# Product 7 on the second Strassen level in two layers, and the first layer's value bias joined at its products

## The chip, the cores and the metric

The kernel runs on one core of one Trainium2 chip. Its engines work side by side, each through its own queue in order: TensorE (PE) multiplies matrices, VectorE (DVE), ScalarE (ACT) and GpSimd (POOL) work elementwise, and SyncE (SP) issues most DMA transfers. POOL issues the DMAs that add to what lies in DRAM. Matmul results land in PSUM, eight banks of 128 partitions by 512 float32 each; DVE and ACT read them out, POOL works in SBUF only.

The metric is the device time of the whole program in microseconds (us).

## The reference

Four layers work on x of shape (128, 64, 512): 128 graphs of 64 nodes with 512 features, all in float32. Each layer adds an attention over the graph's adjacency to x:

```python
h = maximum(layernorm(x), 0); x = x + L0(h, adj, Wq, bq, Wk, bk, Wv, bv)          # 8 heads of 64, softmax
h = maximum(layernorm(x), 0); x = x + L1(h, adj, Wq, bq, Wk, bk, Wv, bv, Wo, bo)  # the same, with an output product
h = maximum(layernorm(x), 0); x = x + L2(h, adj, Wq, Wk, Wv)                       # no softmax: scores masked, rows normed
h = maximum(layernorm(x), 0); x = x + L3(h, w_qkv, w_proj, b_proj, gamma, beta, adj)  # softmax, output product o, then o + layernorm(o)

# inside L0
q, k, v = x @ Wq + bq, x @ Wk + bk, x @ Wv + bv        # (n, 512) by (512, 512)
weights = softmax(q k^T / 8 + mask)                     # each row sums to one
out     = weights @ v
```

In layer 2 the products by Wq and Wk are folded into one 512 x 512 matrix a2 = Wq^T Wk ahead of time.

## The kernel before

**Tiles.** The 8192 rows are cut into NB = 16 blocks of T = 512 rows. The loop `for n in range(N)` near the end runs over N = 64 block-layers: n // 16 is the layer l, n % 16 the block k. A block is normed (`layer_norm`), turned so that features lie on partitions (`turn`: an ACT copy into a z tile that splits 32-bit words into halves, a DMA transpose on SP, an ACT copy back), and multiplied by the layer's weights (`projection`). Attention (`scores`, `attend`, `values`) or, in layer 2, `relate` follows, and x is stored.

**Products.** Each 512 x 512 x 512 product is done by Strassen's method in Winograd's form: the operands are cut into 2 x 2 quarters, eight additions make sums of quarters, and seven products replace eight. The weights' sums are made once a layer (`sums_w`), the block's sums once a block (`sums_x`, four POOL additions 512 wide into a tile S; SO for the output products). A first-level product, of 256 x 256 x 256, is four matmuls of 128 x 128 weights by 256 columns (`prod_T`, `prod_N`).

Some of the seven products are cut once more (`prod_2`): seven matmuls of 128 by 128 in place of four of 256. Which ones is the string that `finer` returns. Before, `LEVEL2` says "423" (products 4, 2 and 3) in layers 0, 1 and 3 from block 2 on, and "43" for the two products of layer 2, a2 and v2, which become "423" (`DEEP`) from block 2 of that layer. Each such product needs four more POOL additions 128 wide for the block (`sums_q`, whose results go to the list `room`) and four for the weight (`sums_q_w`; `deepen` calls it after block 1 of layer 2).

**How a projection runs.** `ORDERS` lists the steps. A number is a first-level product, a number in quotes the part of a deeper one that gathers in its own quarter, and "a", "b", "c" are the second-level terms that several quarters share. "423" runs as

```python
"423": (1, 5, 6, "a", 7, "b", "2", "c", "4", "3"),
"4237": (1, 5, 6, "7", "t", "a", "A", "2", "b", "B", "4", "c", "C", "3"),
```

The second line is already in the program, with the steps that it calls: "7" is three matmuls, "t" one whose result ACT copies to a tile p5 and POOL adds to a 256-wide pair, "A", "B" and "C" one each, which DVE adds 256, 256 and 512 wide. The results gather in PSUM banks named S, 5, T and 2; "A", "B" and "C" use a further one, D. DVE and ACT bring them to the result tile (qT, kT, v, xo), and POOL adds the p5 tiles. A bias is joined there: "col" by ACT's activation, "row" by a DVE add in place of the ACT copy for three quarters and a POOL add (`gps.tensor_tensor(Y[4], Y[4], wide(0), ALU.add)`) for the fourth. Layer 3's output product uses "row".

**Biases outside the products.** In layer 0 the value bias isn't added to v: since attention weights sum to one it is added to the residual, by four POOL additions 512 wide a block in `load_xo`. Layer 1's bo and layer 3's beta are held as a row on all partitions in SBUF and added to DRAM by POOL's accumulating DMAs, 1 MB a block (`adds`, `add_out`). These are the groups x<-row and out_dram<-row of the profile.

**Order.** Nothing is issued as it is written. Every call goes to a `Plan`, which records reads, writes and an estimated duration (`duration`) and then lists the steps by a simulation of the five queues and the eight banks (`order`): of the ready steps the one that could start first, ties by a rank from due times, moved by `PREFER`, a table of offsets in ns by kind of step. `HASTE` moves forward every step that reads a PSUM bank. `issue` emits the list, and so all instructions carry line 316 in the profile. The tables do not change what is computed.

**Buffers.** `Ring` hands out tiles in turn: z has 5, row 3, mx and sr 4, the p1 pool one tile a tag, S and hT two. A step that writes a tile waits for the last reader of what was in it.

Of the kernel before, what the change touches and what calls it, by code (L numbers as in the profile page):

```python
# [19 lines left out]
P = 128  # L20
G = 64
D = 512
# [319 lines left out]
class Pool:  # L342
# [34 lines left out]
ROOM = 5  # L377
DEEP = "423"
# [3 lines left out]
HASTE = 24970.0  # L382
# [5 lines left out]
    "gps dma_start out_0_dram<-row 2048": -808,  # L388
    "gps dma_start out_0_dram<-xo 2048": 3553,
    "gps dma_start x1<-kT 2": -2080,  # L390
    "gps dma_start x1<-row": 2529,
    "gps dma_start x1<-row 2": -1234,
    "gps dma_start x1<-xo": -129329,
    "gps dma_start x1<-xo 2": -25864,
    "gps memset mhalf<- 8": -5457,
    "gps tensor_scalar nb<-mv 4": 11572,
    "gps tensor_scalar nb<-mv 4 2": 33294,
    "gps tensor_scalar ve<-mv 1": -1763,
    "gps tensor_scalar ve<-mv 4": 11580,
    "gps tensor_scalar ve<-mv 4 2": -7060,  # L400
    "gps tensor_tensor S2<-S 128 2": 22107,
    "gps tensor_tensor S2<-S2 128": -559,
    "gps tensor_tensor S2<-S2 128 2": -54598,
    "gps tensor_tensor S2<-hT 128": 2551,
    "gps tensor_tensor S<-S 128": 1168,
    "gps tensor_tensor S<-S 128 2": 2476,
    "gps tensor_tensor S<-S 512": -597,
    "gps tensor_tensor S<-S 512 2": -7501,
    "gps tensor_tensor S<-hT 512": -24545,
    "gps tensor_tensor S<-hT 512 2": -3927,  # L410
    "gps tensor_tensor SO2<-SO 128": 4667,
    "gps tensor_tensor SO2<-SO 128 2": 15658,
    "gps tensor_tensor SO2<-SO2 128": 1209,
    "gps tensor_tensor SO2<-SO2 128 2": -10461,
    "gps tensor_tensor SO<-SO 128": -707,
    "gps tensor_tensor SO<-SO 128 2": -1689,
    "gps tensor_tensor SO<-SO 512": 11408,
    "gps tensor_tensor SO<-SO 512 2": 15673,
    "gps tensor_tensor SO<-oT 512": 1784,
    "gps tensor_tensor SO<-oT 512 2": 15975,  # L420
    "gps tensor_tensor hT<-hT 128": -1135,
    "gps tensor_tensor hT<-hT 128 2": 6337,
    "gps tensor_tensor kT<-kT 128": -30776,
    "gps tensor_tensor kT<-kT 128 2": -14217,
    "gps tensor_tensor kT<-kT 256": -12126,
    "gps tensor_tensor kT<-kT 256 2": -509,
    "gps tensor_tensor kT<-kT 512": 4991,
    "gps tensor_tensor nb<-nb 4": 378,
    "gps tensor_tensor nb<-nb 4 2": -22779,
    "gps tensor_tensor oT<-S 128 2": -2719,  # L430
    "gps tensor_tensor oT<-oT 128": -16598,
    "gps tensor_tensor oT<-oT 128 2": -20,
    "gps tensor_tensor qT<-qT 128": -1109,
    "gps tensor_tensor qT<-qT 128 2": -14844,
    "gps tensor_tensor qT<-qT 256": 8338,
    "gps tensor_tensor qT<-qT 256 2": 167,
    "gps tensor_tensor rn<-ss 8 2": 1409,
    "gps tensor_tensor row<-hT 128": -710,
    "gps tensor_tensor row<-row 128": 14918,
    "gps tensor_tensor rs<-ve 1": 27672,  # L440
    "gps tensor_tensor rs<-ve 4": 5403,
    "gps tensor_tensor rs<-ve 4 2": 2490,
    "gps tensor_tensor s<-hT 128 2": -24185,
    "gps tensor_tensor s<-s 1024": -91676,
    "gps tensor_tensor s<-s 128 2": -19641,
    "gps tensor_tensor v<-v 128": -3704,
    "gps tensor_tensor v<-v 128 2": -9488,
    "gps tensor_tensor v<-v 256": 1526,
    "gps tensor_tensor v<-v 256 2": 1506,
    "gps tensor_tensor w<-w 128": 28546,  # L450
    "gps tensor_tensor w<-w 128 2": 70002,
    "gps tensor_tensor w<-w 256": 2007,
    "gps tensor_tensor w<-w 512": 32937,
    "gps tensor_tensor w<-w 512 2": -1787,
    "gps tensor_tensor xo<-xo 128": 11193,
    "gps tensor_tensor xo<-xo 512": -37778,
    "sca activation kT<-mm 128": -29215,
    "sca activation kT<-mm 256": -3927,
    "sca activation qT<-mm 128": -74377,
    "sca activation qT<-mm 256": -3915,  # L460
    "sca activation s<-s 1024": 194087,
    "sca activation s<-s 256 2": -2224,
    "sca activation xin<-xin 512": 64227,
    "sca activation xin<-xin 512 2": -27076,
    "sca copy hT<-hp 1024": -91399,
    "sca copy hT<-hp 1024 2": 12660,
    "sca copy hT<-mm 512": 2537,
    "sca copy kT<-mm 128": -1201,
    "sca copy kT<-mm 128 2": 12050,
    "sca copy kT<-mm 256": 22596,  # L470
    "sca copy kT<-mm 512": 1630,
    "sca copy oT<-mm 512": 2583,
    "sca copy p5<-mm 128": -33327,
    "sca copy p5<-mm 128 2": -16443,
    "sca copy qT<-mm 128": 636,
    "sca copy qT<-mm 128 2": -1473,
    "sca copy qT<-mm 256": 1288,
    "sca copy qT<-mm 256 2": 7745,
    "sca copy qT<-mm 512 2": 1688,
    "sca copy s<-hp 1024": 10152,  # L480
    "sca copy s<-mm 512": 13393,
    "sca copy v<-mm 128": 2212,
    "sca copy v<-mm 128 2": -451,
    "sca copy v<-mm 256": -5758,
    "sca copy v<-mm 256 2": 10701,
    "sca copy v<-mm 512": 101913,
    "sca copy w<-mm 128": -125,
    "sca copy w<-mm 256": 8826,
    "sca copy xo<-mm 128": 19831,
    "sca copy xo<-mm 256": 6884,  # L490
    "sca copy xo<-mm 512": -3273,
    "sca copy z<-hp 1024": 9089,
    "sca copy z<-mm 512": 225,
    "sca copy z<-oT 1024": -34277,
    "sca copy z<-s 1024": 915,
    "sca copy z<-xin 1024": 71282,
    "sca copy z<-xin 1024 2": -375,
    "syn dma_start a2d<-z": 5859,
    "syn dma_start adj2<-in_adj_dram": -1388,
    "syn dma_start bk0<-in_L0_gnn_bk_dram": -130,  # L500
    "syn dma_start bk1<-in_L1_gnn_bk_dram": 5273,
    "syn dma_start bq0<-in_L0_gnn_bq_dram": 15019,
    "syn dma_start bq1<-in_L1_gnn_bq_dram": -1693,
    "syn dma_start bv1<-in_L1_gnn_bv_dram": -4763,
    "syn dma_start hp<-z": 10021,
    "syn dma_start hp<-z 2": -14842,
    "syn dma_start oT<-in_L2_gnn_Wq_dram": 7116,
    "syn dma_start oT<-in_L2_gnn_Wv_dram": 12239,
    "syn dma_start out_0_dram<-qT": -11288,
    "syn dma_start out_0_dram<-xo 2": 3308,  # L510
    "syn dma_start qT<-out_0_dram": -19349,
    "syn dma_start row<-in_L0_gnn_bv_dram": -4082,
    "syn dma_start row<-in_L1_gnn_bo_dram": 830,
    "syn dma_start row<-in_L3_gnn_b_proj_dram 2": 19121,
    "syn dma_start row<-in_L3_gnn_ln_gamma_dram 2": 15560,
    "syn dma_start w<-a2d": -573,
    "syn dma_start w<-in_L0_gnn_Wk_dram": 825,
    "syn dma_start w<-in_L0_gnn_Wq_dram": 17643,
    "syn dma_start w<-in_L0_gnn_Wv_dram": -7702,
    "syn dma_start w<-in_L1_gnn_Wo_dram": 2537,  # L520
    "syn dma_start w<-in_L1_gnn_Wq_dram": 10058,
    "syn dma_start w<-in_L1_gnn_Wv_dram": 14266,
    "syn dma_start w<-in_L3_gnn_w_proj_dram": 5411,
    "syn dma_start w<-in_L3_gnn_w_qkv_dram 2": 21150,
    "syn dma_start x1<-xo": -11230,
    "syn dma_start xin<-out_0_dram": -1632,
    "syn dma_start xin<-out_0_dram 2": -15870,
    "syn dma_start xin<-x1": -4553,
    "syn dma_start xo<-in_x_dram": 2298,
    "syn dma_start xo<-x1 2": 13243,  # L530
    "ten matmul mm<-S 128": 12919,
    "ten matmul mm<-S 128 2": 8018,
    "ten matmul mm<-S 256": 6187,
    "ten matmul mm<-S 256 2": -3891,
    "ten matmul mm<-SO 128": 3732,
    "ten matmul mm<-SO 128 2": 2595,
    "ten matmul mm<-SO 256": 281,
    "ten matmul mm<-SO 256 2": 3959,
    "ten matmul mm<-hT 128": 7158,
    "ten matmul mm<-hT 128 2": -5677,  # L540
    "ten matmul mm<-hT 256": 3637,
    "ten matmul mm<-hT 256 2": -7222,
    "ten matmul mm<-hT 64 2": 14063,
    "ten matmul mm<-oT 128": -2756,
    "ten matmul mm<-oT 256": -147,
    "ten matmul mm<-oT 256 2": -4195,
    "ten matmul mm<-oT 512": -5757,
    "ten matmul mm<-qT 64": 14482,
    "ten matmul mm<-row 128 2": -6474,
    "ten matmul mm<-s 128 2": 5537,  # L550
    "ten matmul mm<-s 256": 11122,
    "ten matmul mm<-s 256 2": 9177,
    "ten matmul mm<-s 64": 5357,
    "ten matmul mm<-v 64": -17945,
    "ten matmul mm<-v 64 2": -283,
    "ten matmul mm<-w 128": -1300,
    "ten matmul mm<-w 256": -118,
    "ten matmul mm<-w 256 2": 57,
    "ten transpose mm<- 128": 1068,
# [1172 lines left out]
```

## Time and profile before

| | before |
|---|---|
| median of 3 runs | 2752.95 us (2752.92 to 2753.37) |
| the profiled execution, its own time | 2752.1 us |
| its span | 2750.3 us |
| granted clock of TensorE | 0.999 |
| POOL, 16 DMAs x<-row (bo) of 1 MB, issue to landing | 13.9 us |
| POOL, 15 DMAs x<-xo of 1 MB, issue to landing | 9.2 us |
| SP, 444 transposes hp<-z, issue to landing | 3.3 us |
| ACT copies p<-mm 128 wide, 398 | 275 ns each |
| ACT copies v<-mm 512 wide, 194 | 596 ns each |
| DVE adds v<-mm,v 256 wide, 122 | 412 ns each |
| DVE adds v<-mm,v 512 wide, 314 | 687 ns each |

The span runs from the first instruction to the last one's end in the trace; what lies around it (1.8 us) belongs to the program's own time. PEld is TensorE's weight load, which overlaps its matmuls. POOL's records overlap each other by some 0.1 to 0.2 us, so what one of its instructions costs is read from start to start: four in a row, 128 wide, start at 1102.65, 1103.07, 1103.48 and 1103.90 us, 0.41 us apart, and two 256 wide take 1.40 us. A layer fills some 690 us of the span: the third starts at about 1461 us.

### The profile page before, as it was taken

The page shows a single profiled execution, that of the slowest core. Times are in us where ns is not written, and L with a number is a line of the kernel's source. Part 1 is how long each engine was busy: PE and PEld are TensorE (multiplying, and loading weights), DVE is VectorE, ACT ScalarE, POOL GpSimd, SP SyncE. Part 2 cuts the span into 40 slices and gives each one's busy share as a digit, 9 for nine tenths or more (in the row PEclk, how much of TensorE's full clock was granted, in tenths as well). Part 3 has the DMA queues.
Part 4 walks back from the last instruction along what each step waited for, and adds up shares of the span by engine and source line. Part 5 has one row for each costly group of instructions (what it writes and reads, how often), then busy time and mean ns, then how long its engine had stood idle before and what let it go on. Part 6 is the DMA issues. An engine that isn't in the chain of part 4 may idle for free.

```text
span 2750.3 us, 72249 instructions
## 1 busy us (share of the span) xinstructions
PE 2734.5 (99%) x29427; PEld 2506.0 (91%) x29427; DVE 1735.3 (63%) x3298; ACT 1897.0 (69%) x3169; POOL 2102.2 (76%) x2915
## 2 busy tenths in 40 slices
PE   9999999999999999999999999999999999999998
PEld 8999899999999999999999898989999999999997
DVE  6666566665656556556555555555577677677777
ACT  6788688888776766766766666665766666666662
POOL 5667778779978778778689866656887887887885
PEclk9999999999999999999999999999999999999999
DMA  5666576666465556465575856567544664754644
GB/s 143 157 149 133 148 151 146 154 143 164 80 124 110 93 115 110 94 115 107 97 150 123 179 146 169 151 154 181 113 90 81 119 114 78 127 105 84 130 88 97
DMA packets 635021, 344.50 MB, mean 125 GB/s; under 512 B 484288, under 2 KB 565952, under 8 KB 634688
## 3 DMA queue, kind: packets, MB, share of 16 engines
q1 hardware_dynamic: 601424, 273.83, 43.9%
q0 software_dynamic: 33264, 66.06, 14.7%
q8 instruction: 230, 3.77, 0.6%
q14 instruction: 103, 0.84, 0.1%
HBM read 120.63 MB, written 102.76 MB: 81 GB/s over the span
## 4 chain that ended last, share of the span: by engine, by line
PE 89%; POOL 6%; ACT 2%; DVE 1%; DMA 1%; issue 1%; SPq 0%; POOLq 0%; ACTq 0%; DVEq 0%
PE mm L316 89%; POOL w L316 2%; POOL s L316 1%; POOL S L316 1%; DMA hp<-z 1%; POOL SO L316 0%; ACT z L316 0%; ACT s L316 0%; DMA x<-xo 0%; ACT xin L316 0%; POOL xo L316 0%; ACT kT L316 0%; DVE st L316 0%; DVE sr L316 0%; POOL v L316 0%
## 5 line engine op out<-in xcount | busy, mean ns | idle before, releaser
L316 PE MATMUL mm<-S,w 128*128 128x256 f32 (+1 forms) x4516 | 900.1, 338 | 1.6 <-issue 1.0
L316 PEld LDWEIGHTS mm<-S,w 128*128 128x128 f32 x4516 | 734.5, 191 | 62.5 <-POOL S L316 1.0
L316 PE MATMUL mm<-hT,w 128*128 128x128 f32 (+1 forms) x3364 | 593.3, 307 | 0.8 <-ACT p L316 0.7
L316 PEld LDWEIGHTS mm<-hT,w 128*128 128x128 f32 x3364 | 509.8, 191 | 39.9 <-ACT p L316 1.4
L316 PE MATMUL mm<-w,S 128*128 128x256 f32 (+1 forms) x2520 | 514.9, 340 | 0.0
L316 DVE TENSOR_TENSOR kT<-mm,kT 128x256 f32<-128x256 f32 (+1 forms) x433 | 258.9, 612 | 317.1 <-PE mm L316 190.6
L316 PEld LDWEIGHTS mm<-w,S 128*128 128x128 f32 x2520 | 418.8, 191 | 42.0 <-ACT s L316 3.1
L316 DVE TENSOR_TENSOR v<-mm,v 128x512 f32<-128x512 f32 (+2 forms) x440 | 264.3, 607 | 232.1 <-PE mm L316 132.5
L316 DVE TENSOR_TENSOR qT<-mm,qT 128x512 f32<-128x512 f32 (+2 forms) x440 | 264.6, 609 | 196.7 <-PE mm L316 149.3
L316 ACT COPY hT<-hp 128x1024 uint16<-128x1024 uint16 x252 | 337.5, 1362 | 14.7 <-DMA hp<-z 14.3
L316 ACT COPY v<-mm 128x128 f32<-128x128 f32 (+1 forms) x380 | 172.2, 455 | 234.8 <-PE mm L316 205.4
L316 PE MATMUL mm<-w,hT 128*128 128x128 f32 (+1 forms) x1844 | 326.7, 307 | 1.1 <-DVE p L316 0.7
L316 PEld LDWEIGHTS mm<-w,hT 128*128 128x128 f32 x1844 | 277.8, 191 | 19.4 <-ACT s L316 0.9
L316 POOL TENSOR_TENSOR S<-hT 128x512 f32<-128x512 f32 (+1 forms) x172 | 196.3, 1219 | 104.8 <-ACT hT L316 104.8
L316 ACT COPY z<-xin 128x1024 uint16<-128x1024 uint16 x252 | 260.4, 1080 | 0.0
L316 POOL TENSOR_TENSOR qT<-qT,p 128x256 f32<-128x256 f32 (+1 forms) x184 | 118.0, 651 | 185.4 <-DVE qT L316 105.4
L316 PE MATMUL mm<-w,SO 128*128 128x256 f32 (+1 forms) x1302 | 259.1, 335 | 0.0
L316 ACT COPY s<-hp 128x1024 uint16<-128x1024 uint16 x188 | 253.0, 1373 | 1.6 <-DMA hp<-z 1.5
L316 POOL TENSOR_TENSOR s<-s,mx 128x1024 f32<-128x1024 f32 x96 | 208.5, 2221 | 40.9 <-DVE mx L316 40.7
L316 PEld LDWEIGHTS mm<-w,SO 128*128 128x128 f32 x1302 | 210.0, 191 | 16.8
L316 PE MATMUL mm<-w,oT 128*128 128x128 f32 (+1 forms) x1252 | 222.3, 303 | 0.2 <-ACT oT L316 0.2
L316 ACT COPY z<-s 128x1024 uint16<-128x1024 uint16 x188 | 193.7, 1053 | 39.5 <-POOL s L316 39.5
(125 smaller groups left out, 4811.5 us busy)
## 6 DMA issues: line engine op xcount, KB each, us to landing
xin<-x SPq DMA_DIRECT2D x128, 256.0 KB, 3.8
xin<-in_x_dram SPq DMA_DIRECT2D x64, 256.0 KB, 4.0
x<-row POOLq DMA_DIRECT2D x16, 1024.0 KB, 13.9
xin<-out_dram SPq DMA_DIRECT2D x64, 256.0 KB, 3.5
out_dram<-row POOLq DMA_DIRECT2D x16, 1024.0 KB, 13.9
x<-xo POOLq DMA_DIRECT2D x15, 1024.0 KB, 9.2
out_dram<-xo POOLq DMA_DIRECT2D x15, 1024.0 KB, 9.9
xo<-in_x_dram SPq DMA_DIRECT2D x32, 256.0 KB, 4.2
```

Of the source, the lines that this page charges most:

```text
L316: getattr(getattr(self.nc, eng), op)(*a, **k)
```

## The change

- **Product 7 deeper.** `DEEP` becomes "4237" and `finer` returns it for q1, k1, v1, a2 and v2 from block 2 of their layer on. Layers 0 and 3 and the output products keep "423".
- **Room for its sums.** `sums_x` hands out a second tile of eight 128-wide slots beside S (five before). `deepen` takes a tile for the weight's three sums, from a new ring w7 of two, or from the row ring for v1, and is now called in layer 1 too, after block 1. It makes the sums of product 7 (in layer 2 of products 2 and 7).
- **p5.** The tile of product 7 shares its buffer with that of product 2.
- **Layer 0's value bias** is passed to the projection as "row"; the four additions in `load_xo` are gone.
- **bo and beta** are no longer held in SBUF: the accumulating DMAs read them from DRAM, repeated over partitions.
- **Rings.** z goes from 5 tiles to 4, row from 3 to 2, mx and sr from 4 to 2; `fold`, which makes a2, uses the tiles of SO in place of z.
- **Order.** `PREFER` is replaced, with separate offsets for the four layers (before: layer 2 apart from the rest), and `HASTE` goes from 24970 to 60319. The other constants of the plan stay.

```diff
-ROOM = 5
-DEEP = "423"
+ROOM = {"S": 8, "SO": 5}
+DEEP = "4237"
+DEEPER = ("q1", "k1", "v1", "a2", "v2")
+LENT = ("v0", "v1")
...
-HASTE = 24970.0
+HASTE = 60319.0
...
-    zs, hps = pool("zs", 5), pool("hps", 4)
-    rows = pool("rows", 3)
-    sm = pool("sm", 4)
+    zs, hps = pool("zs", 4), pool("hps", 4)
+    rows, w7 = pool("rows", 2), pool("w7", 2)
+    sm, sm2 = pool("sm", 4), pool("sm2", 2)
...
     def finer(name, n):
-        if name[1] == "2" and n >= 2 * NB + 2:
+        if name in DEEPER and n % NB >= 2:
             return DEEP
...
-    def deepen(name, at):
-
-        if "rooms" not in W2:
-            W2["rooms"] = p1.tile([P, KC * KC, P], F32, tag="SO", name="rooms")
-        for i, q in enumerate("75"):
-            W2[name][q] = W2["rooms"][:, at + 3 * i : at + 3 * i + 3]
+    def deepen(name):
+
+        if name in LENT:
+            W2[name]["7"] = rows.tile([P, KC, P], F32, tag="row", name=f"w7_{name}")
+        else:
+            W2[name]["7"] = w7.tile([P, 3, P], F32, tag="w7", name=f"w7_{name}")
         for q in DEEP:
             if q not in LEVEL2[name]:
                 sums_q_w(name, q, gps.tensor_tensor)
...
-            f = zs.tile([P, D], F32, tag="z", name=f"fa_{dc}")
+            f = p1.tile([P, ROOM["SO"], P], F32, tag="SO2", name=f"fa_{dc}")[:, :KC].rearrange("p c f -> p (c f)")
...
-        if 3 * len(parts) > len(room):
-            more = (p2 if tag == "S" else p1).tile([P, ROOM, P], F32, tag=f"{tag}2", name=f"{nm}2")
-            room = room + [more[:, i] for i in range(ROOM)]
+        if 3 * len(parts) >= len(room):
+            more = (p2 if tag == "S" else p1).tile([P, ROOM[tag], P], F32, tag=f"{tag}2", name=f"{nm}2")
+            room = room + [more[:, i] for i in range(ROOM[tag])]
...
-            p5[q] = p1.tile([P, P], F32, tag=f"p5_{q}", name=f"p5_{q}_{nm}")
+            p5[q] = p1.tile([P, P], F32, tag=f"p5_{2 if q == '7' else q}", name=f"p5_{q}_{nm}")
...
-            mx = sm.tile([P, NS], F32, tag="mx", name=f"mx_{n}")
+            mx = sm2.tile([P, NS], F32, tag="mx", name=f"mx_{n}")
...
-        if l in xo_row:
-            row = R[xo_row[l]]
-            for t in range(NT):
-                gps.tensor_tensor(xos[n][:, t, :], xos[n][:, t, :], row, ALU.add)
-                if t < NT - 1:
-                    yield 1
         ready.add(("xo", n))
...
-            R["b1"] = row_bc("b1", bo1)
+            R["b1"] = bo1.partition_broadcast(P)
...
-            R["bp"], R["gam"], R["bet"] = row_bc("bp", bp3), row_bc("gam", gam3), row_bc("bet", bet3)
+            R["bp"], R["gam"], R["bet"] = row_bc("bp", bp3), row_bc("gam", gam3), bet3.partition_broadcast(P)
...
+            if k == 1 and f"q{l}" in DEEPER:
+                deepen(f"q{l}")
...
-            run(projection(prod_N, f"v{l}", xop, f"v_{n}", v))
+            run(projection(prod_N, f"v{l}", xop, f"v_{n}", v, (R["b0"][:, :H2], R["b0"][:, H2:]) if l == 0 else None))
+            if k == 1 and f"v{l}" in DEEPER:
+                deepen(f"v{l}")
```

## The prediction

> **What bounds the kernel now.** I read the busy times first, then the slices, the chain that ended last and TensorE's own waits. From the page:
>
> ```profile
> PE 2734.5 (99%) x29427; PEld 2506.0 (91%) x29427; DVE 1735.3 (63%) x3298; ACT 1897.0 (69%) x3169; POOL 2102.2 (76%) x2915
> PE   9999999999999999999999999999999999999998
> PEclk9999999999999999999999999999999999999999
> PE 89%; POOL 6%; ACT 2%; DVE 1%; DMA 1%; issue 1%; SPq 0%; POOLq 0%; ACTq 0%; DVEq 0%
> ```
>
> TensorE (PE) is busy in every slice at the full clock, and the chain is 89% matmul. Span less busy time is 2750.3 - 2734.5 = 15.8 us. The windows put 2.1 us of that into the first 43 us and 10.9 us into the last 86 us; only 2.8 us lies in between. Busy matmuls are modelled, so I ask next who ever kept PE waiting (engine <- what it waited for: us in total, times, longest):
>
> ```profile
> PE mm L316 <- issue: 1.5, 2, 1.0
> ...
> PE mm L316 <- DVE v L316: 1.0, 2, 0.7
> PE mm L316 <- DVE p L316: 0.7, 1, 0.7
> ...
> PE mm L316 <- POOL S L316: 0.6, 2, 0.4
> ```
>
> Almost nothing. So the time is the number of matmuls times their spacing, and an edit gains what it takes from PE unless it makes a wait that today doesn't exist. The spacing is read off the timeline of PE in the second layer, start against start (start us, us, ...):
>
> ```profile
> 901.81 1.89 PE L316 MATMUL mm<-S,w 128*128 128x256 f32 x8
> 903.54 0.83 PE L316 MATMUL mm<-hT,w 128*128 128x128 f32 x6
> 904.21 0.39 PE L316 MATMUL mm<-S,w 128*128 128x128 f32 x2
> 904.43 0.61 PE L316 MATMUL mm<-hT,w 128*128 128x128 f32 x4
> 904.88 0.39 PE L316 MATMUL mm<-S,w 128*128 128x128 f32 x2
> 905.10 0.39 PE L316 MATMUL mm<-hT,w 128*128 128x128 f32 x2
> 905.32 1.89 PE L316 MATMUL mm<-S,w 128*128 128x256 f32 x8
> ```
>
> One float32 matmul shows as two records. Eight records 256 wide, one first-level product of four matmuls, take 903.54 - 901.81 = 1.73 us (216 ns a record). The next 16 records 128 wide take 905.32 - 903.54 = 1.78 us (111 ns each).
>
> **Part 1, product 7 one level deeper.** It holds for q1, k1, v1, a2 and v2 in the 14 blocks of a layer with k >= 2: 14 x 5 = 70 projections; the other three second-level products are there already. Each loses 8 records of 216 ns (1.73 us) and gains 7 matmuls, 14 records of 111 ns (1.56 us): 0.167 us. **70 x 0.167 = 11.7 us less on PE**, which is on the path throughout.
>
> Two rules of the Trainium skill are weighed here. "TensorE: Matmul & The Clock Gate", section LDWEIGHTS, prices a weight load by its columns, 128 / 1.2 = 107 ns, whatever the rows. That is a floor which a half-wide matmul meets and a 256-wide one doesn't, and the row stands just above it: 111 ns, not half of 216. Counting multiplications alone, seven eighths of 1.73 us, would give 0.216 us, 15.1 us in all. I take the row. "Perfetto Trace Analysis", section Identifying the Most-Contended Engine, speaks against the change: matmul busy time is a poor judge because matmuls are pipelined, and the load share should be read. There the change adds 70 x 6 = 420 loads. In the load rows of the same layer eight take 1.60 us, while six and eight together take 0.75 + 0.97 = 1.72, so the load time would grow by 0.12 x 70 = 8 us. By that reading it would be a loss of 8 us. But the starts of the matmuls already contain whatever the loads cost, so the start spacing decides.
>
> What this adds beside PE, per deeper projection: on DVE adds A and B, 256 wide, and C, 512 wide: 2 x 0.41 + 0.68 = 1.50 us (105 us in all, at v<-mm,v); on ACT one 128-wide copy of 0.28 (20 us, at p<-mm); on POOL one 256-wide add, 0.70 start to start (49 us, at v<-v,p). Once a block POOL makes product 7's four input sums, 128 wide, 0.41 apart: 28 x 1.65 = 46 us. The weights' sums are 20 such instructions, 8 us. None is on the path while its engine keeps up. For a middle block of the second layer, and for the three stretches around the turn to the third:
>
> ```profile
> 1117.00:1160.00 43.00, 43.00 (x505) 39.91 (x504) 26.36 (x48) 27.35 (x47) 36.78 (x51) 1.00 0.59 114
> ...
> 1418.00:1461.00 43.00, 42.25 (x496) 38.82 (x495) 25.48 (x46) 26.57 (x46) 36.97 (x48) 1.00 0.85 177
> 1461.00:1504.00 43.00, 42.96 (x426) 39.23 (x425) 19.47 (x40) 24.34 (x41) 42.74 (x70) 1.00 0.49 110
> 1504.00:1547.00 43.00, 42.57 (x425) 37.33 (x423) 20.82 (x50) 26.88 (x44) 42.01 (x67) 1.00 0.92 179
> ```
>
> After the window's length come PE, loads, DVE, ACT, POOL. POOL's mean over the 15 windows from 773 to 1418 is 33.0 of 43. The second layer adds 1.65 + 3 x 0.70 = 3.75 a block, 36.8 of 42.5, or 87%; DVE goes from 25.3 to 29.8. The third layer has POOL at about 27 and gets 3.05. Both engines still fit, so inside the layers I cost this at nothing: PE's own queue hides it. At the turn it isn't free. POOL is full for 86 us, PE already loses 0.75 + 0.04 + 0.43 = 1.2 us there, and 7.5 us of sums from the two blocks ahead and 4.1 us from the weights of a2 and v2 come on top. If POOL's order puts the urgent sums first it costs 0; if all 11.6 us is in PE's way, 11.6. I take 1.5, near the 1.2 that a full POOL costs today.
>
> A fifth PSUM bank (D) is open beside S, 5, T and 2, of eight, and "t" opens T sooner. The trace has no row for it; the nearest is PE's whole wait for drains, the DVE and ACT lines of which sum to 2.6 us for all projections. Bounds: 0, or 0.1 us a projection, 7 us. I take 0.5.
>
> The tile p5 of product 7 is now that of product 2: ACT's copy for "2" waits until POOL's "t" add has read it. PE issues "a", "A" and "2" between, 9 matmuls or 2.0 us; the add takes 0.7. Two softmax subtractions ahead of it on POOL take 3.8, so ACT may stand for some 2 to 3 us, with the drains of other banks queued behind it. ACT is at 69% and the banks cover one such wait: 0, inside the bank bound above.
>
> **Part 2, first layer's value bias.** From the groups of POOL and DVE by form (x count | busy us, mean ns):
>
> ```profile
> L316 POOL TENSOR_TENSOR xo<-xo,row 128x512 f32<-128x512 f32 x64 | 81.4, 1286 | 0.1
> ...
> L316 POOL TENSOR_TENSOR kT<-kT,row 128x512 f32<-128x512 f32 x14 | 17.9, 1279 | 1.1
> ...
> L316 DVE TENSOR_TENSOR kT<-mm,row 128x512 f32<-128x512 f32 x42 | 28.5, 680 | 0.0
> ```
>
> The 64 adds go: 81 us off POOL. The fourth layer's output product has the same bias path already, 42 DVE adds and 14 POOL adds, and shows the price: POOL +14 x 1.28 = 18 us; DVE +50 x 0.68 = 34 us (three a block, four in the first two); ACT -50 x 0.60 = 30 us. On PE nothing, as in the fourth layer. POOL is relieved by 3.8 us a block just where it is full before the second layer (42.84 and 41.84 in the windows from 645 to 730), and PE's losses there, 0.10 + 0.07 + 0.71, may halve: **-0.4**. The 12 weight sums of q1, k1, v1 follow a block later, 5 us, where POOL has 8 us free.
>
> **Part 3, buffers and constants.** z goes from 5 to 4. A norm's four transposes write z some 1.4 us apart, and a transpose lands 3.3 us after issue, so four suffice if SP is prompt; otherwise ACT waits a microsecond, covered by its 31%. mx and sr have two tiles for two uses a block: 0. bo1 and the beta row are added from DRAM instead of SBUF, 32 transfers of 1 MB. The row shows 13.9 us from SBUF; no row shows DRAM to DRAM with one repeated source row. Between 0 and twice the landing time; the sums are read 16 blocks later, so 0, except for transposes that are slowed. fold's copies wait for their DMAs in turn (2.5 us each), early in layer one: 0.
>
> **Part 4, the order.** It holds the same work; ends and stalls can go either way. Below: all 2.8 us of middle stalls and 1.5 us of the tail, 4.3 us gained. Above: a just-in-time chain that slips (first rival). I take 0.
>
> **Sum.** -11.7 + 1.5 + 0.5 - 0.4 = -10.1 us. Against the profiled execution, 2752.1 us (span 2750.3 and 1.8 around it), that makes 2742.0; the median of the runs is 0.85 above it, 2752.95 - 10.1 = **2742.8 us**.
>
> **Rivals.** *POOL's sums come late (the slower side).* POOL's timeline in a second-layer block:
>
> ```profile
> 1120.43 1.28 POOL L316 TENSOR_TENSOR S<-hT 128x512 f32<-128x512 f32 x1 [3.53 <-ACT hT L316]
> ...
> 1138.02 4.00 POOL L316 TENSOR_TENSOR s<-s,mx 128x1024 f32<-128x1024 f32 x2
> ```
>
> From the arrival of hT to the start of the next block POOL works without a gap; one block earlier its last input sum starts at 1103.90, after that block's first product (1102.05). The change puts 1.65 (sums) + 0.70 (k) + 0.70 (v) = 3.05 us into that stretch, and product 7 now wants its sums about 5 us into a block. If the norm doesn't move forward, PE stands 3.05 us in each of the 14 blocks: +43, 2784 us. From 0.8 us a block (11.7 / 14) the gain is gone; beyond 1.2 it is slower. Against it: POOL sits idle some 10 us in the same block before hT, waiting for ACT, and the norm depends only on an x that was loaded long before. 12%, with half of it slower and most of the rest within 0.2%.
>
> *The turn to the third layer takes the gain:* 6 to 9 us of the 11.6 in PE's way: 2747 to 2750, say 2748.5. For it: POOL full for two blocks. Against: POOL has 15 us free in the next block, and later weights can wait. 8%.
>
> *The order also clears the stalls:* -11.7 - 4.3, 2737. 6%.
>
> *The change doesn't shorten PE*, because loads bind (the second rule above): 2753 to 2761. The start spacing excludes it nearly: 2%.
>
> **Chances.** The forecast, new stalls of at most 4 us, has 72%. What a measurement of this kernel can tell from no change is 0.2%, 5.5 us. Faster: 72 + 6 and small shares of the two stall rivals, 81%; same 12%; slower 7%. The range leaves out the late sums above and the cleared order below: 2737 to 2751.
>
> **What would show it.** Right: 70 x 6 = 420 more PE records, PE busy lower by 11 to 12 us, waits of PE still a few us, POOL in the second layer at 36 to 37 of 42.5. Wrong: PE waiting for POOL S or ACT p once a block; 128-wide records spaced 124 ns apart (14 of them then take the 1.73 us of a first-level product); POOL's turn leaving PE idle by several us.

## The result, and the profile after

The changed kernel takes **2773.32 us** (median of 4 runs, 2773.04 to 2785.53) beside 2752.93 us for the kernel before, run next to it: a ratio of 1.0086, 95% interval [1.0058, 1.0113]. It is 20.4 us slower where 10.1 us less was forecast. Its profiled execution took 2773.25 us, with a span of 2771.4 us, 21.1 us longer than before.

The page of the changed kernel: busy times, the slices of TensorE and its clock, and the chain that ended last by engine.

```profile
PE 2734.8 (99%) x29847; PEld 2515.7 (91%) x29847; DVE 1878.8 (68%) x3558; ACT 1886.9 (68%) x3189; POOL 2158.9 (78%) x3067
PE   9999999999999999999999999999999999999997
PEclk9999999999999999999999999999999999999999
PE 87%; POOL 6%; ACT 3%; issue 1%; DVE 1%; DMA 1%; SPq 0%; POOLq 0%; ACTq 0%; DVEq 0%
```

There are 420 more PE records, as forecast, yet PE's busy time is the same (2734.5 before). Idle time went from 15.8 to 36.6 us. The forty slices of 69 us show neither. TensorE's waits in the changed kernel (engine and line <- what it waited for: us in total, times, longest):

```profile
PE mm L316 <- issue: 8.0, 3, 4.9
PE mm L316 <- DVE v L316: 7.3, 3, 5.4
PE mm L316 <- POOL s L316: 4.9, 1, 4.9
...
PE mm L316 <- POOL S L316: 0.7, 1, 0.7
```

Three stalls, 15.2 us together, make up most of the increase, one under each of the first three names. "POOL S", the wait that my slower rival was built on, is 0.7 us. The same windows that were shown of before, and the two that hold the other stalls (length, then PE, loads, DVE, ACT, POOL, clock, DMA share, GB/s):

```profile
1117.00:1160.00 43.00, 43.00 (x511) 39.76 (x510) 30.25 (x55) 29.16 (x53) 36.36 (x48) 1.00 0.71 124
1418.00:1461.00 43.00, 36.74 (x460) 33.85 (x460) 23.11 (x42) 19.78 (x39) 31.07 (x45) 0.92 0.91 148
1461.00:1504.00 43.00, 42.40 (x428) 38.84 (x427) 20.67 (x43) 32.25 (x49) 41.68 (x58) 1.00 0.49 99
1547.00:1590.00 43.00, 37.13 (x323) 33.66 (x322) 22.90 (x51) 24.17 (x41) 34.64 (x58) 0.92 0.81 168
2707.00:2750.00 43.00, 36.03 (x454) 33.19 (x454) 30.02 (x52) 11.73 (x26) 26.00 (x32) 0.92 0.55 83
```

In the middle of the second layer PE reads as full and POOL as 36.4 of 43. Most of the idle time lies in three windows, where PE stands for 6 to 7 us and the granted clock is 0.92 as well. Before, the window at 1547 was full (the one at 2707 holds the end of that program and can't be compared):

```profile
1547.00:1590.00 43.00, 43.00 (x355) 38.93 (x352) 24.73 (x61) 25.25 (x44) 31.24 (x49) 1.00 0.72 183
```

The second line of the changed kernel shows POOL far from full (31.07 of 43) at the turn where I had expected it to be late. The large DMA share (0.91) points elsewhere. From the page's table of DMA issues (KB each, median us from issue to landing):

```profile
x<-in_L_gnn_bo_dram POOLq DMA_DIRECT2D x16, 1024.0 KB, 17.7
...
out_dram<-in_L_gnn_ln_beta_dram POOLq DMA_DIRECT2D x16, 1024.0 KB, 18.2
x<-xo POOLq DMA_DIRECT2D x15, 1024.0 KB, 9.3
```

The two bias transfers took 13.9 us from their SBUF row; the repeated DRAM row takes 17.7 and 18.2. The other accumulating transfers are as before (9.2).

**The stall at 1447 us.** PE's timeline in the changed kernel (start us, us):

```profile
1446.68 0.60 PE L316 MATMUL mm<-w,SO 128*128 128x256 f32 x2
1452.14 2.72 PE L316 MATMUL mm<-w,SO 128*128 128x256 f32 x6 [4.86 <-issue]
```

The eight matmuls of one first-level product stop after two. No data are missing, since operands and bank are those of the two before. What PE lacks is instructions. The DMA view of the changed kernel has a queue for them, whose 234 packets carry 3.83 MB, 16 KB each. PE has 2 x 29847 records of matmul and load, so a packet holds some 255 of them. The DMA view in two stretches of the stall, 1446.0 to 1448.6 us and 1448.6 to 1450.7 us (queue, kind: packets, MB, share of 16 engines):

```profile
q1 hardware_dynamic: 295, 0.07, 105.8%
q0 software_dynamic: 95, 0.19, 39.8%
```

```profile
q1 hardware_dynamic: 725, 0.18, 164.0%
q0 software_dynamic: 20, 0.03, 7.5%
q8 instruction: 1, 0.02, 5.8%
```

In the first stretch, in which PE comes to a stand (1447.28), POOL's accumulating transfers (q0) and SP's transposes (q1) fill the engines. The instruction packet moves only in the second: it lands at 1450.63 and PE goes on 1.5 us later. At 1341 and 2719 us PE also resumes 1.5 us after such a packet lands (1342.16 and 1343.63; 2722.18 and 2723.73). All three stalls follow a burst of 128 matmuls of 64 by 64, which uses up 256 instructions, a whole packet, in 2.1 us. The stall that the waits put down to "POOL s" (2719) is therefore taken as one of these too: the matmul that stands there, mm<-w,oT, does not read s.

SP's transposes wait at the same place. All of them in the changed kernel, the issuing instruction's duration and then the landing (min/median/max):

```profile
L316 SPq DMA_TRANSPOSE hp<-z x444: 1231/1260/9847, 41.9 to 2687.5; - x148
...
DMA to landing us min/median/max: 3.0/3.3/20.3
```

And before:

```profile
L316 SPq DMA_TRANSPOSE hp<-z x444: 1231/1269/4358, 35.2 to 2671.7; - x148
```

The median is unchanged, but the longest issue is 9.8 us (4.4 before), and three of them hold SP for 19 us at 1427, behind x<-xo and the bias transfer that POOL issued at 1427.06 and 1429.95.

**The stall at 1567 us** is another kind. DVE and then PE in the changed kernel:

```profile
1567.22 0.88 DVE L316 SCALAR_TENSOR_TENSOR xo<-mm,rn,xo 128x256 f32<-128x256 f32 x2 [4.26 <-DMA xo<-x]
```

```profile
1572.35 0.79 PE L316 MATMUL mm<-w,s 128*128 128x128 f32 x2 [5.41 <-DVE v L316]
```

PE waits for DVE to empty a bank, and DVE, in order, stands behind a load of x. The new order issues these loads at 1558 to 1565 us, right beside the accumulating transfer x<-kT (1558.54). Before, the loads of xin went out at 1517.4, ahead of x<-kT at 1524.5.

**Why PE's busy time didn't fall.** Five-microsecond windows after the stall at 1447:

```profile
1450.00:1455.00 5.00, 2.86 (x8) 2.30 (x8) 0.52 (x1) 1.06 (x1) 2.75 (x3) 0.63 1.16 246
1455.00:1460.00 5.00, 5.00 (x32) 4.97 (x31) 1.03 (x3) 0.55 (x3) 0.47 (x2) 0.69 0.54 194
```

The clock is 0.63 and then 0.69: (0.37 + 0.31) x 5 = 3.4 us of clock are missing, and as much behind the stalls at 1567 (0.58 and 0.74) and 2719 (0.60 and 0.71). In the trace's clock record each is a stretch of 6.83 us at 0.50, part of which passes while PE still stands. Of the three, 6.0, 5.2 and 4.1 us lie under running matmuls, and half of that, 7.7 us, shows as longer matmuls. So PE's work is 2734.8 - 7.7 = 2727.1 us, 7.4 less than before. The rest of what product 7 took off PE is in pauses that the view of waits doesn't list (behind experiment 1).

A stall's length is here and below PE's idle time in the timeline's rows; the expectations count some of them 0.3 to 0.4 us longer.

### The profile page after: what moved, and what is told of

Its sections match the earlier page's. It is cut to its first block, busy times and chain, and to the rows that moved or that the text cites. A ratio compares the mean times of both kernels' runs of the same rounds, so it can differ in the third digit from the quotient of the medians.

```text
span 2771.4 us, 73691 instructions
## 1 busy us (share of the span) xinstructions
PE 2734.8 (99%) x29847; PEld 2515.7 (91%) x29847; DVE 1878.8 (68%) x3558; ACT 1886.9 (68%) x3189; POOL 2158.9 (78%) x3067
## 3 DMA queue, kind: packets, MB, share of 16 engines
q8 instruction: 234, 3.83, 0.6%
## 4 chain that ended last, share of the span: by engine, by line
PE 87%; POOL 6%; ACT 3%; issue 1%; DVE 1%; DMA 1%; SPq 0%; POOLq 0%; ACTq 0%; DVEq 0%
PE mm L316 87%; POOL s L316 1%; POOL S L316 1%; ACT z L316 1%; POOL SO L316 1%; DMA hp<-z 1%; ACT xin L316 1%; DMA xin<-x 1%; POOL w L316 0%; POOL kT L316 0%; POOL x L316 0%; POOL oT L316 0%; POOL v L316 0%; ACT qT L316 0%; ACT kT L316 0%
## 5 line engine op out<-in xcount | busy, mean ns | idle before, releaser
L316 PE MATMUL mm<-S,w 128*128 128x256 f32 (+1 forms) x4740 | 910.4, 328 | 2.3 <-ACT kT L316 1.4
L316 PEld LDWEIGHTS mm<-S,w 128*128 128x128 f32 x4740 | 750.7, 191 | 61.4 <-ACT kT L316 1.6
L316 PEld LDWEIGHTS mm<-hT,w 128*128 128x128 f32 x3364 | 504.7, 191 | 36.7 <-ACT hT L316 2.4
L316 DVE TENSOR_TENSOR kT<-mm,kT 128x512 f32<-128x512 f32 (+1 forms) x475 | 283.7, 604 | 263.5 <-PE mm L316 153.3
L316 DVE TENSOR_TENSOR qT<-mm,qT 128x512 f32<-128x512 f32 (+2 forms) x524 | 303.6, 593 | 204.6 <-PE mm L316 92.3
L316 DVE TENSOR_TENSOR v<-mm,v 128x512 f32<-128x512 f32 (+1 forms) x524 | 306.3, 593 | 143.4 <-POOL v L316 50.8
L316 ACT COPY v<-mm 128x512 f32<-128x512 f32 (+1 forms) x330 | 141.7, 429 | 189.5 <-PE mm L316 167.8
L316 POOL TENSOR_TENSOR qT<-qT,p 128x256 f32<-128x256 f32 (+1 forms) x212 | 149.9, 709 | 148.5 <-DVE qT L316 82.5
L316 POOL TENSOR_TENSOR s<-s,mx 128x1024 f32<-128x1024 f32 x96 | 192.7, 2081 | 46.1 <-DVE mx L316 45.9
## 6 DMA issues: line engine op xcount, KB each, us to landing
x<-in_L_gnn_bo_dram POOLq DMA_DIRECT2D x16, 1024.0 KB, 17.7
out_dram<-in_L_gnn_ln_beta_dram POOLq DMA_DIRECT2D x16, 1024.0 KB, 18.2
```

The costliest lines, as they stand in the source:

```text
L316: getattr(getattr(self.nc, eng), op)(*a, **k)
```

## The experiments

**1. The changed kernel without the bias transfers.** bo and beta are left out; all else, the order too, is the changed kernel's.

```diff
+                if "accum_op" in k and ("bo_dram" in a[1].tensor.name or "beta_dram" in a[1].tensor.name):
+                    continue
```

> The changed kernel with the 32 accumulating transfers of bo and beta left out (both are zero), every other instruction in the same order. Theory A, the transfers read their bias from DRAM, run longer and hold up what shares the DMA engines (TensorE's instructions, loads of x): the three stalls of about 5 us at 1447, 1567 and 2718 us and the 2.8 us at 1341 go, with the halved clock behind them, 2741 to 2749 us. Theory B, the new order put loads and transposes where they collide, whatever the bias reads: 2765 to 2773. Theory C, POOL's added sums come late: 2773.

Measured: 2746.61 us (2743.35 to 2749.13), ratio to before 0.9976 [0.9967, 0.9986]. The transfers cost the changed kernel 26.7 us, more than its whole loss. Both programs issue the same matmuls in the same order, so the traces can be set side by side matmul by matmul; what the changed kernel loses against this one, by stretch of this one's span (worked out from the start times of the two traces):

```
0 to 112 us        +1.8
112 to 615          0.0
615 to 1318        +6.7   second layer, 0.1 to 0.5 us at a time
1318 to 1410       +1.4
1410 to 1508       +8.7   turn to the third layer (stall at 1447)
1508 to 1616       +2.4   both have a stall here
1616 to 2651       +0.1
2651 to the end    +5.6   (stall at 2719)
```

The second layer's 6.7 us stand under no name in PE's waits, since a matmul's modelled end covers pauses this short. In the two traces, most of the matmuls that start later there than they do here start 0.03 to 0.04 us after a semaphore that they wait for: ACT's for 4.8 us of the 6.7, as ACT frees a bank. In eight blocks running it is the same two places, 0.19 us each. ACT is late there because POOL is. POOL in one block of the changed kernel, and then of this run:

```profile
927.45 1.31 POOL L316 DMA_DIRECT2D x<-xo  x1
928.32 1.75 POOL L316 DMA_DIRECT2D x<-in_L_gnn_bo_dram  x1
...
937.75 2.13 POOL L316 TENSOR_TENSOR s<-s,mx 128x1024 f32<-128x1024 f32 x1
```

```profile
922.06 1.30 POOL L318 DMA_DIRECT2D x<-xo  x1
...
931.48 1.90 POOL L318 TENSOR_TENSOR s<-s,mx 128x1024 f32<-128x1024 f32 x1 [0.16 <-DVE mx L318]
```

PE is 5.1 us behind this run at that place, POOL's softmax subtraction 6.3. So issuing the bias transfer makes POOL about 1.2 us late in the block, and ACT, which exponentiates what POOL subtracted, as late with the banks behind it. The source of the bias plays no part: experiments 5 to 8 lose 6.5 to 7.0 us in the same stretch. In the kernel before, where POOL has 3.75 us less to do in a block by the forecast's count, the transfers cost PE 0.0 us from 900 to 1400 us (its trace beside that of experiment 2). This is read from traces; no run moved POOL's work.

**2. The kernel before without them.** The same omission of bo and beta in the kernel before.

> The kernel before without its 32 bias transfers (bo and beta, both zero), all else in its order. It is what the transfers cost there when they read SBUF. Theory A (the DRAM source is the cost, not the transfers): 2749 to 2753 us. If the transfers as such cost much: 2740 or less, and then the 26.7 us between the changed kernel and the changed kernel without them is not the source's alone.

Measured: 2746.6 us (2745.6 to 2749.35), ratio 0.998 [0.9972, 0.9987]. Here they cost 6.0 us. So 26.7 - 6.0 = 20.7 us of the change's +20.4 come through these transfers; without them the two kernels are equal. The first lines of both pages, without the transfers, before and then changed, and a late window of the changed one:

```profile
PE 2731.9 (99%) x29427; PEld 2505.0 (91%) x29427; DVE 1735.1 (63%) x3298; ACT 1900.3 (69%) x3169; POOL 2065.9 (75%) x2883
```

```profile
PE 2724.8 (99%) x29847; PEld 2512.8 (92%) x29847; DVE 1876.4 (68%) x3558; ACT 1893.3 (69%) x3189; POOL 2121.2 (77%) x3035
```

```profile
2720.00:2725.00 5.00, 5.00 (x76) 4.37 (x69) 1.66 (x3) 2.15 (x4) 1.36 (x1) 0.66 0.24 25
```

Now PE's busy time falls, by 7.1 us, though the second figure has slow clock in it: behind a stall of 4.12 us at 1550 (0.76 and 0.56 in the windows there), and again near the end (0.66 above). Together 8.9 us of matmuls ran at half the clock, 4.4 us more than they take at the full one. The work itself fell by 11.5 us. Idle time rose from 14.1 to 19.8 us.

**3. The DRAM row alone, in the kernel before.**

```diff
+                if "accum_op" in k and a[1].tensor.name.startswith("row"):
+                    src = self.bias[a[0].tensor.name.startswith("out")]
+                    a = [a[0], src.partition_broadcast(P).unsqueeze(1).to_broadcast([P, NT, D])]
```

> The kernel before in its own order, with only the source of the bias transfers changed from the SBUF row to DRAM. Theory A: 2758 to 2775 us, with new waits of TensorE that end on nothing shown (issue). Theory B and C: 2753 us, within 3.

Measured: 2780.41 us (2776.14 to 2783.79), ratio 1.0098 [1.0082, 1.0113]. One source address, and nothing else of the change, costs 27.7 us. The transfers land in 17.9 and 17.7 us. The same place in the kernel before and then here:

```profile
2692.22 0.72 PE L316 MATMUL mm<-S,w 128*128 128x128 f32 x5
2693.94 0.27 PE L316 MATMUL mm<-S,w 128*128 128x128 f32 x1 [1.00 <-issue]
```

```profile
2706.18 0.72 PE L319 MATMUL mm<-S,w 128*128 128x128 f32 x5
2713.45 0.37 PE L319 MATMUL mm<-S,w 128*128 128x128 f32 x1 [6.54 <-issue]
```

PE stops between the same two matmuls. Before, it stood 1.0 us for its instruction packet; behind the longer transfer it stands 6.5 us, and the window from 2710 to 2720 has a clock of 0.53. The wait of 1.0 us stood in the profile of before, under "issue".

**4. Rows of their own, in the kernel before.** The same transfers read 1 MB of DRAM, written once early, in which each of the 512 rows has its own copy (the rows copied hold the values of bo and beta).

```diff
+                self.nc.sync.dma_start(
+                    self.zeros.rearrange("t p d -> p t d"), self.row.unsqueeze(1).to_broadcast([P, NT, D])
+                )
...
+                    a = [a[0], self.zeros.rearrange("t p d -> p t d")]
```

> The kernel before in its own order, the bias transfers reading from 1 MB of DRAM in which every 2 KB row is a row of its own (zeros, written once early), instead of one row read 512 times. If the repeated row is what is slow: transfers land in about 14 us again, 2753 us within 4. If any DRAM source is: about 18 us to landing and 2772 to 2785 us as with the repeated row.

Measured: 2752.96 us (2752.0 to 2755.6), ratio 1.0002 [0.9993, 1.0011]; landing 14.0 and 13.9 us. So DRAM as a source is as good as SBUF. What is slow is 512 reads of one 2 KB row.

**5. The changed kernel with the bias from SBUF.** It reads the rows of two other biases, which hold the same values and lie in SBUF at that time (all but two of the bo transfers, and all of beta's).

```diff
+                    if beta or i not in self.late:
+                        a = [a[0], (self.bprow if beta else self.b0row).unsqueeze(1).to_broadcast([P, NT, D])]
```

> The changed kernel in its own order, with the bias transfers reading from a row in SBUF of the same values (zeros) in place of DRAM, except the last two of bo (at 1430 and 1537 us), for which no row is free. Theory A: the stalls at 1341 and 2718 us go, those at 1447 and 1567 stay: 2773 - 2.8 - 8.5, about 2762 us. Theory B and theory C: 2773 us.

Measured: 2766.31 us (2762.82 to 2771.52), ratio 1.0049 [1.0034, 1.0064]. Only 7.0 of the 26.7 us come back: the stall at 2719 is gone, those at 1341 (2.77), 1448 (2.40) and 1563 (6.04) are not. The last two stand behind the two bo transfers that still read DRAM, so what SBUF as their source would do there isn't seen; the next experiment has no such exception.

**6. The changed kernel with rows of their own in DRAM.**

```diff
+                    self.nc.sync.dma_start(self.own[b][t], self.rows[b].partition_broadcast(P))
...
+                    a = [a[0], self.own["beta_dram" in a[1].tensor.name].rearrange("t p d -> p t d")]
```

> The changed kernel in its own order; bo and beta are first spread to 1 MB of DRAM each (every row a row of its own, early, in quarters) and the 32 bias transfers read from there. If the repeated row is what the change lost: transfers land in about 14 us, the stalls on issue go, and the time is that without bias transfers plus the 6 us they cost the kernel before: 2746.6 + 6 = about 2752.6, between 2749 and 2756 us. If the new order can't bear bias transfers of any kind: 2762 or more.

Measured: 2763.58 us (2757.29 to 2766.15), ratio 1.0036 [1.0024, 1.0048]; landing 13.9 and 14.0 us. It gains 9.7 us. Left are stalls of 3.33 us at 1340, 2.26 at 1449 and 3.77 at 1565. In the new order the transfers are dear without the repeated row too.

**7. The same, and x<-kT 10 us later**, to take it away from the loads of x at 1565.

```diff
+        for i in [i for i in todo if "accum_op" in self.steps[i][1][0][2] and self.steps[i][1][0][1][1].tensor.name.startswith("kT")]:
+            todo.remove(i)
+            todo.insert(next(j for j, u in enumerate(todo) if self.start[u] >= self.start[i] + 10000), i)
```

> The same, and the last accumulating transfer of the second layer (x<-kT) issued 10 us later, behind the loads of x that VectorE waits for and ahead of the next block's (25 us later it met those). If the meeting of the two makes the stall at the turn: 4.5 to 6 us of it and 3.4 us of halved clock go, 2742 to 2747 us. If not: the same as the run beside it, within 3 us.

Measured: 2758.63 us (2753.42 to 2765.97), ratio 1.002 [1.0013, 1.0026]. The stall at 1565 is gone, and 5.0 us with it. Those at 1339 (3.34) and 1448 (2.52) remain, both under "issue".

**8. The same, and one pair of accumulating transfers 8 us later**, the pair issued at 1333 us.

```diff
+        i = [i for i in todo if "accum_op" in self.steps[i][1][0][2]][12]
+        todo.remove(i)
+        todo.insert(next(j for j, u in enumerate(todo) if self.start[u] >= self.start[i] + 8000), i)
```

> The run with own rows and the output add 10 us later, and with one more move: the pair of accumulating transfers (output and bias of one block) that was issued at about 1333 us is issued 8 us later. Theory: the stall of 3.6 us at 1339 us is TensorE's own fetch of instructions, 16 KB after a burst of 128 short matmuls, queued behind that pair; with the pair away the stall falls under 1 us and the time by 3.6 us of idle and some 1.5 us of slower clock, to 2753.5 (2751.5 to 2755.5). Rival: the stall belongs to the fetch alone, whatever lies beside it: stall and time stay, 2758.6 (2757 to 2760).

Measured: 2758.25 us, ratio 1.001 [1.0002, 1.0018]. Windows at that place in experiment 7, and then here:

```profile
1340.00:1350.00 10.00, 7.57 (x44) 6.94 (x45) 4.55 (x8) 2.16 (x5) 7.89 (x7) 0.83 0.56 102
```

```profile
1340.00:1350.00 10.00, 9.74 (x108) 9.03 (x99) 7.71 (x13) 2.69 (x5) 10.00 (x10) 1.00 0.85 137
```

At its place the theory holds: the stall and its slow clock are gone, and from 1324 to 1393 us the second trace gains 4.25 us on the first. The time doesn't follow. In the profiled execution the next fetch stall grew from 2.52 to 3.28 us, start and end took 2.6 us more between them, and the span is only 1.2 us shorter. The 14 executions lie apart, four at 2750.1 to 2751.5 and ten at 2757.0 to 2761.2. What the four escaped isn't seen, as none of them was profiled.

**9. The changed kernel without bias transfers, x<-kT 25 us later.** Experiment 1 with this one move; bo and beta are left out.

> The changed kernel without bias transfers (2746.6 us), and the last accumulating transfer of the second layer (x<-kT, 1 MB) issued 25 us later. Theory B for the one stall that is left (4.5 us at 1549 us, VectorE standing for loads of x and xo): the transfer went out with those loads in the new order, so the stall and the halved clock behind it go, -8 us: 2737 to 2741 us. If the loads are late for another reason: 2745 to 2748.

Measured: 2747.53 us (2742.08 to 2749.24), ratio 0.9978 [0.9971, 0.9986]: nothing gained. x<-kT, now issued at 1564.74, meets the next block's loads; the stall moves from 1550 to 1574 and is 5.87 us long. PE's busy time is 2723.6 us, of which half the clock made 3.0, so its work is 11.3 us below experiment 2.

**10. Each bias transfer in two halves**, 10 and 22 us later, from the DRAM row, with x<-kT 25 us later.

```diff
+                        for x in range(2):
+                            at = slice(2 * x, 2 * x + 2)
+                            late.append((self.start[i] + 10000 + 12000 * x, [v[:, at] for v in a], k))
```

> The changed kernel with DRAM as the source, but each bias transfer in two halves, 10 and 22 us after its place (the last two of beta stay), and x<-kT 25 us later. If the length for which the DMA engines are filled without a gap is what starves TensorE: most stalls go, 2745 to 2755 us. If what counts is the traffic read from DRAM, wherever it lies: 2762 or more.

Measured: 2843.3 us (2835.5 to 2847.88), ratio 1.0331 [1.0312, 1.035], 70 us worse than the change. PE's waits:

```profile
PE mm L330 <- ACT xo L330: 15.7, 12, 3.1
PE mm L330 <- DVE v L330: 9.0, 14, 4.1
```

The halves land in 8.7 and 8.1 us but now meet the blocks' transposes. ACT's wait for those of the scores was 0.9 us in the changed kernel, and is here:

```profile
ACT s L330 <- DMA hp<-z: 40.1, 18, 3.6
```

Each half is an issue of its own in POOL's queue as well; how the 70 us divide between the two was not measured. The order's own places for the transfers were better than these.

**11. The changed kernel under the old order**: the old PREFER, HASTE and phases.

> The changed kernel with the old table of preferences, the old HASTE and the old two phases; product 7, the bias edits and the buffers as changed. Theory A: no better than the changed kernel by more than a few us, 2765 to 2785, since DRAM remains the source. Theory B: 2742 to 2755 us. Theory C: 2773 or more.

Measured: 2904.8 us (2896.42 to 2909.03), ratio 1.0546 [1.0527, 1.0566]. PE waits for "ACT v" 36.7 us in 29 places and for "DVE v" 32.1 in 32. The other parts need a new order: the old table costs them 131 us more than the new one.

**12. The kernel before with the bias added by DVE**, one add of 2048 columns a block ahead of the sum's own transfer; the last block's beta keeps its transfer.

```diff
+                    if not a[1].tensor.name.startswith("row"):
+                        row = self.brow[beta].unsqueeze(1).to_broadcast([P, NT, D])
+                        self.nc.vector.tensor_tensor(a[1], a[1], row, ALU.add)
+                    elif not beta or a[0].offset != 3932160:
+                        continue
```

> The kernel before with the bias (the output projection's, and beta) joined to the block's sum by one VectorE instruction ahead of the accumulating transfer, in place of a transfer of its own (the last block's beta keeps its transfer). Theory, that these transfers cost the kernel before some 6 us by what they crowd out: 6.0 us gone, and 2.2 us of VectorE a block lie beside other work, as VectorE is busy for some 63% of the span: 2747 to 2750. Rival: VectorE's added instruction stands ahead of a normalisation or an eviction that TensorE waits for, 0.2 to 0.5 us in each of 31 blocks: 2753 to 2763.

Measured: 2797.73 us (2795.71 to 2799.8), ratio 1.0158 [1.0145, 1.0171]. DVE's group of these adds (busy us, mean ns), and PE's first two waits:

```profile
L318 DVE TENSOR_TENSOR xo<-xo,row 128x2048 f32<-128x2048 f32 x30 | 71.9, 2397 | 0.1
```

```profile
PE mm L323 <- DVE kT L323: 17.0, 13, 1.6
PE mm L323 <- ACT xo L323: 15.6, 12, 1.3
```

DVE is 65% busy over the span, but one instruction of 2.4 us in its queue makes the next eviction late: the two waits are 25 in number and 1.3 us each in the mean. The rival was right and its price too low: 43.7 us lost and the 6.0 saved are 1.6 us in each of 31 blocks, where it had 0.2 to 0.5. The order doesn't know of this add; a plan that did might place it better, which was not tried.

No version that computes everything beat the kernel before.

## Why the prediction was wrong

**What failed is Part 3's zero for bo and beta from DRAM.** It bounded the landing ("between 0 and twice the landing time") and then argued by the reader: "the sums are read 16 blocks later, so 0, except for transposes that are slowed". The landing rose by 4 us, well inside the bounds, and the sums were indeed in time. But the transfer's reader isn't the only one it can delay. While it runs, every other user of the 16 DMA engines queues beside it, and PE depends on three of them: its own instruction packets, the loads of x that DVE stands behind, and the transposes. Its issue also stands in POOL's queue. The transfers cost 6.0 us before and 26.7 after (experiments 1 and 2): the term was +20.7, not 0. The exception that I named in half a sentence was not priced.

What of it is the row and what the order can't be split once and for all. In the old order the repeated row alone costs 27.7 us (3). In the new one giving it rows of its own returns 9.7 (6), x<-kT away from the loads 5.0 more (7), and 12.0 lie between that and no bias transfers at all (1). Set beside each other, the traces of 7 and 1 put 6.5 us into the pauses behind POOL along the second layer and 9.1 into the two stretches with the fetch stalls at 1339 and 1448; 3.2 go the other way, as experiment 1 still has the stall at 1550.

**Part 1** was right in its main term: -11.7 forecast, -11.5 and -11.3 measured as PE work (experiments 1 and 9 against 2, less the slow clock). POOL's use in the second layer was right too, 36.2 of 43 in the mean. That it costs nothing, as "PE's own queue hides it", holds without bias transfers. With them, POOL's added work and their issue together make the 6.7 us of pauses, a small form of my slower rival. The load-share rule as I applied it, which spoke of a loss of 8 us, is refuted by the same numbers: PEld rose by 6 to 8 us and PE's work fell. Its slips in the sums change little: the rows shown, unrounded, give -12 for the main term, the eight weight sums at the turn take 3.3 us and not 4.1, and POOL's 33.0 was of 43 us, not of 42.5.

**The turn, +1.5 and +0.5.** Even without bias transfers the product's gain is given back: idle time +5.7 and slow clock +4.4 in experiment 1 against 2, some 10 us, of which the stall at 1550 makes 6.9 (4.12 idle and 2.7 of slow clock). That this is near the 6 to 9 us of my second rival is chance, as its cause is another. I looked for POOL's sums; POOL has 12 us free at the turn. The stall comes from the new order's x<-kT beside the loads of x (moved away, it went in experiment 7, and moved onto the next loads, it followed in 9). This belongs to **Part 4**, whose "0" counted engines and left the DMA queues out.

**Part 2, -0.4**: PE's losses in the three windows that it named went from 0.88 to 0.44. Right in size, though POOL stays full in the first two (42.8 of 43), with other work, so the relief that it argued from isn't seen.

**The rivals.** POOL's late sums (12%), 3.05 us a block, did not happen (0.7 us under "POOL S"); PE not shortened (2%) did not either; the cleared order (6%) is the reverse of what happened. The true case, a transfer off the path that takes from PE what it needs to run, had no rival and no share in the range. Without bias transfers -11.5 and +10.1 make -1.4 in the profiled executions and 0.0 in the medians, and 20.7 on top is about the measured 20.4.

## What to carry to other kernels

A transfer whose result nobody waits for still costs what it crowds out: before costing it at nothing, list who shares the DMA engines while it runs (instruction packets after a burst of short matmuls, loads that an in-order engine stands behind, transposes) and what stands behind its issue in the queue, and look for "issue" waits of PE, which even at 1 us mark a place without slack. Don't repeat one DRAM row as the source of a large accumulating transfer; copy it out once. Where PE is at 99%, count a stall of 3 us or more with the slow clock behind it, and look for pauses that its waits don't list by setting two traces side by side.

## What the runs showed of the hardware

- **A repeated DRAM row** of 2 KB, read 512 times by an accumulating transfer of 1 MB, takes 17.7 to 18.6 us to land; with rows of their own, or from SBUF, 13.8 to 14.4 (medians of the runs).
- **TensorE's instructions** come in packets of 16 KB over the same DMA engines. A packet that is late stops PE for 1.0 to 6.5 us here, and PE resumes 0.9 to 1.6 us after it lands.
- **POOL's queue** holds the issue of an accumulating transfer: with one more of them, what follows in the block shown was about 1.2 us late.
- **The clock after a stall** goes to 0.50. Ahead of a program's end, every such stretch in these traces lasts 3.41 us or a multiple of it. Behind 6.5 us of standing (experiment 3) it was 10.2 us, behind 4.1 to 6.0 us (experiments 1, 5 and 9, and three times in the changed kernel) 6.8, behind 3.3 to 3.8 us (experiments 6 to 8) 3.4. Below that the length doesn't decide it: of seven stalls of 2.3 to 2.8 us two were followed by a slow stretch, and one of 1.11 us near the end was in experiments 1, 5 and 8 but not in 6, 7 and 9. The Trainium skill's "TensorE: Matmul & The Clock Gate", Part 1 on the clock gate, has half the clock after an idle window of about 3.4 us and the full one after a busy window of that length. The slow stretches agree with it; that 2.5 us of standing, and 1.1, were enough in some runs is below its figure.
